# The eight products of a context group tied together, in a masked attention kernel

## The chip, the cores and the metric

The kernel runs on one core of one Trainium2 chip. The time is the device time of an execution in microseconds (us); the number given is the median of several runs. Besides, one execution was profiled.

## The reference

There are 16 batches of 512 features by 1024 tokens. Queries, keys and values are one and the same projection; a token mask removes keys from the softmax, and a masked query attends evenly to everything.

```python
xt = jnp.transpose(x, (0, 2, 1))                       # x: (16, 512, 1024)
q = xt @ Wq.T
qh = q.reshape(B, T, NH, dk).transpose(0, 2, 1, 3)     # NH = 8, dk = 64
scores = scale * jnp.einsum('bhqd,bhkd->bhqk', qh, qh)
logits = (scores * cmask + (1.0 - cmask) * NEG) * rmask
attn = jax.nn.softmax(logits, axis=-1)
ctx = jnp.einsum('bhqk,bhkd->bhqd', attn, qh)
ctx = ctx.transpose(0, 2, 1, 3).reshape(B, T, D)
return x + jnp.transpose(ctx @ Wo.T, (0, 2, 1))
```

## The kernel before

**Compaction.** About half of the tokens of a batch are unmasked. The kernel sorts token numbers into slots, unmasked first, and computes the attention for 544 slots alone: four blocks of 128 and a tail of 32. A masked token's output is the projected mean, which is added to its row elsewhere. Rows come and go by indirect DMAs on POOL's queue (`rows` L335, `scatter_now` L796).

**A batch on TensorE.** Rows are transposed (`xt`, L420) into `pm` tiles; ScalarE (ACT) rounds them to f16 (L380) and VectorE (DVE) takes the remainder (L381). The query projection (`query`, L443) is 12 f16 products for each of 8 tiles; its result is moved out by ACT (L446) and split into f16 halves. `value` (L489) transposes it to values. `scores` (L611) makes for one head and one block of keys a tile `pss` of 128 x 544 in four f16 products, and ACT turns it into the exponentials `p` with their sums (L615). The scores of the 32 tail slots are made for four heads at once (L586): 16 products whose weights are 32 columns wide, each head in a strip of its own of the array, followed by one exponential (L590), a split on DVE and transfers into `pt`. `attend` (L629) multiplies the exponentials with the values in f32: for a pair of heads and a block of keys four products, each 64 columns wide, the two heads in the two halves of the array. The tail's part of the context (L632) is four products at full width, after which ACT copies `pav` out (L636). `recip_rows` (L665) transposes the reciprocal sums into a `pm` tile, from which they go through DRAM to the rows of `rb`; `norm` scales with them, and `project` (L712, L717) makes the output rows.

**PSUM.** There are two buffers for score tiles (`ps_s`), two of the small ones (`ps_m`, whose tiles are `pm`) and one for the context (`ps_av`).

**The order of the work.** `run` writes the work out by hand. The loop runs over the 16 batches; in each there are 18 steps (`S`): 16 pairs (p, i) of a pair of heads p and a block i, and two for the tail. A step issues the scores of two heads, and between them `fill` puts in pieces of a list `m` of other work (transposes, queries and values of the next batch, output projection of the one before), by shares of a planned cost. Context work comes later: after i = 1 and i = 3 the `attend` calls of two earlier steps are made one after the other, the younger first. These are the eight products of a group:

```python
elif i in (1, 3):
    for f in ready[1::-1] + ready[2:]:
        f()
    ready = []
```

This is the order in which instructions are given to a scheduler, which chooses the order on each engine by priorities and by when it holds operands to be ready. The first call of a group begins with `i` odd and with the head k = 1. `behind(ins)` tells the scheduler to issue what is in its scope after `ins`; `high_priority(offset=HPO)`, with HPO = 300, ranks what is in its scope above other work. [...]

Of the kernel before, what the change touches and what calls it, by code (L numbers as in the profile page):

```python
# [23 lines left out]
DK = 64  # L24
# [8 lines left out]
CH = C // 2  # L33
# [13 lines left out]
HPO = 300  # L47


class Fast:  # L50
# [12 lines left out]
    def __init__(self, ctx, tc, x, x_nat, mask_t, wq_t, wo_t, out):  # L63
        self.tc, self.nc = tc, tc.nc
        self.x, self.x_nat, self.out = x, x_nat, out
        self.B = x.shape[0] // T
        pool = lambda name, bufs, **k: ctx.enter_context(tc.tile_pool(name=name, bufs=bufs, **k))
        self.const = pool("const", 1)
        self.one = pool("one", 1)
        self.dram = pool("dram", 8, space=bass.MemoryType.DRAM)  # L70
        self.ps_s = pool("ps_s", 2, space=PS)
        self.ps_av = pool("ps_av", 1, space=PS)
        self.ps_m = pool("ps_m", 2, space=PS)
        self.st = {}
        self.scatters = []
        self.exp, self.pool = [], []

        self.paced, self.beat = False, None
        self.urgent, self.spare = [], []

        self.soon = []
        self.w, self.raw = {}, {}
        self.src = {"q": wq_t, "o": wo_t}
        self.setup(mask_t)
# [535 lines left out]
    def attend(self, b, p, i, ps):  # L620
        nc, s = self.nc, self.st[b]

        if i == 1:
            s["pav"] = self.ps_av.tile([P, 2, 512], F32, tag="av", name="pav")
        for g in range(2):
            for k in (1, 0) if i < 4 else range(2):
                cols = slice(g * CH, (g + 1) * CH)
                if i < 4:
                    nc.tensor.matmul(s["pav"][k * DK:(k + 1) * DK, g, :CH], lhsT=s["v"][p][:, i, k * DK:(k + 1) * DK],  # L629
                                     rhs=ps[k][:, cols], start=(i == 1), stop=False)  # L630
                else:
                    nc.tensor.matmul(s["pav"][:, g, :CH], lhsT=s["vt"][p // 2][:, k, p % 2 * 2:p % 2 * 2 + 2, :],  # L632
                                     rhs=s["pt"][:, p % 2, cols], start=False, stop=(k == 1))
        if i == 4:
            c = self.sb([P, C], F32, "c", 4)
            nc.scalar.copy(c.rearrange("p (g c) -> p g c", g=2), s["pav"][:, :, :CH])  # L636
            s["c"].append(c)
# [192 lines left out]
    def run(self, flag):  # L830
# [7 lines left out]
        def xt(n):  # L838
            return [(0.45, L(self.xt, n, c)) for c in range(4)] + [(0.25, L(self.xt, n, 4))]

        def query(n, e, g):
            u = [(1.37, L(self.query, n, e, g))]
            return u + [(0, L(self.qsplit, n, e))] if g else u

        def value(n, e):
            return [(0.45, L(self.value, n, e))]
# [8 lines left out]
        for i, e in enumerate(ends):  # L855
            g = list(range(ends[i - 1] + 1 if i else 0, e + 1))
# [73 lines left out]
        if True:  # L930
            for b in range(B + 1):
# [18 lines left out]
                if n < B:  # L950
                    q, x, v = (lambda e, g: query(n, e, g)), xt(n)[2 if b == 0 else 0:], (lambda e: value(n, e))
# [19 lines left out]
                    if b == 0:  # L971
                        k = next(k for k, (c, f) in enumerate(m) if f is index[0][1])
# [32 lines left out]
                def fill(part, end=False):  # L1005
                    nonlocal done, goal, pos
                    goal += part * unit
                    while pos < len(m) and (end or (part and done + m[pos][0] / 2 <= goal)):
                        m[pos][1]()
                        done += m[pos][0]  # L1010
                        pos += 1

                for st, (p, i) in enumerate(S):
                    soon, self.soon = self.soon, []
                    for f in soon + free.get(st, []):
                        f()
                    if i is None:
                        self.scores(b, p, None)
                    else:
                        ps = [self.scores(b, 2 * p, i)]  # L1020
                        if i == 2 and whole:
                            whole.pop()()
                    fill(share[st][0], st == N - 1)
                    if i is not None:
                        ps.append(self.scores(b, 2 * p + 1, i))

                    for _ in range(1 if b < B - 2 else -(-len(self.urgent + self.spare) // (N - st))):
                        self.issue()

                    if i in (0, 2):  # L1030
                        ready, todo = todo, []
                    elif i in (1, 3):
                        for f in ready[1::-1] + ready[2:]:
                            f()
                        ready = []
                    fill(share[st][1])
                    if i is not None:
                        todo.append(L(self.attend, b, p, i, ps))
                    if i == 3:
                        (whole if p < 3 else todo).append(L(self.attend, b, p, 4, None))  # L1040
                        if p < 3:
                            free.setdefault(st + 2, []).append(L(self.recip_sums, b, p))
                            free.setdefault(st + 3, []).append(L(self.recip_rows, b, p))
                            if p < 2 or b == B - 1:
                                free.setdefault(min(st + 7, N - 1), []).append(L(self.norm, b, p))
# [148 lines left out]
```

## Time and profile before

| | |
|---|---|
| median of three runs | 1074.26 us (1073.34 to 1080.06) |
| profiled execution | 1082.2 us |
| its span, first to last instruction | 1080.5 us |
| TensorE (PE) busy | 1053.5 us, 98% |
| VectorE (DVE) busy | 739.3 us, 68% |
| ScalarE (ACT) busy | 679.0 us, 63% |
| GpSimd (POOL) busy | 317.5 us, 29% |
| granted TensorE clock, mean | 0.993 |

The profile names a group by source line, engine, operation and tiles (out<-in), with partitions x elements and type; x is the number of records. A record of a f32 context product is half of a product, so the 1024 products of L629 are 2048 records. A length in the timeline is that of a pipelined product from its issue to its end; what a product takes of TensorE is seen from start to next start. Idle time stands with the one who ended it.

### The profile page before, as it was taken

How to read it: one execution, taken by the hardware profiler on the slowest of the kernel's cores; microseconds unless marked ns; L12 is line 12 of the kernel's file. 1: busy time of each engine (PE TensorE's matmuls, PEld its weight loads, DVE VectorE, ACT ScalarE, POOL GpSimd, SP SyncE). 2: the span in 40 equal slices, each digit the busy share in tenths (PEclk: the TensorE clock that was granted, in tenths of full speed). 3: DMA queues.
4: the chain of work that ended last, by engine and by line, in shares of the span. 5: the costliest groups of instructions: out<-in, count | busy, mean ns of one | idle time of the engine just before them, and what ended most of it. 6: DMA issues, size and time to landing. Idle time of an engine off the chain costs nothing.

```text
span 1080.5 us, 23254 instructions
## 1 busy us (share of the span) xinstructions
PE 1053.5 (98%) x8386; PEld 698.3 (65%) x8386; DVE 739.3 (68%) x2375; ACT 679.0 (63%) x1722; POOL 317.5 (29%) x303
## 2 busy tenths in 40 slices
PE   7899999999999999999999999999999999999996
PEld 6566666666666666666666666666666676666553
DVE  5698668676765767767685676958577676757553
ACT  4786667566666756657666666766667565655550
POOL 2101022232401222332322323223232322234643
PEclk8999999999999999999999999999999999999999
DMA  5756565546655654666556566554765555466652
GB/s 186 218 152 167 138 175 157 170 139 191 173 141 156 170 168 145 189 192 172 175 143 194 168 182 188 154 172 134 211 190 171 179 149 154 134 179 195 193 165 85
DMA packets 78122, 181.35 MB, mean 168 GB/s; under 512 B 15008, under 2 KB 16800, under 8 KB 78000
## 3 DMA queue, kind: packets, MB, share of 16 engines
q1 hardware_dynamic: 56816, 111.62, 37.1%
q0 software_dynamic: 21184, 68.18, 19.8%
q8 instruction: 68, 1.11, 0.4%
q14 instruction: 54, 0.44, 0.1%
HBM read 92.34 MB, written 33.91 MB: 117 GB/s over the span
## 4 chain that ended last, share of the span: by engine, by line
PE 88%; DVE 5%; ACT 3%; issue 2%; DMA 1%; POOL 0%; another core or an unknown queue 0%; POOLq 0%; SPq 0%; ACTq 0%; DVEq 0%
PE pav L629 23%; PE pss L611 21%; PE pm L443 15%; PE pm L712 14%; PE pm L420 3%; PE pav L632 3%; PE pm L489 2%; PE pss L586 2%; PE pm L665 1%; ACT p L615 1%; PE pm L511 1%; ACT xm L365 1%; PE warm L303 1%; ACT p L590 1%; DVE p L596 1%
## 5 line engine op out<-in xcount | busy, mean ns | idle before, releaser
L615 ACT ACTIVATE p<-pss,nm 128x544 f32<-128x544 f32 x512 | 365.9, 717 | 231.8 <-PE pss L611 221.8
L611 PE MATMUL pss<-xx 128*128 128x272 f16 x2048 | 314.1, 280 | 3.2 <-ACT p L615 2.3
L629 PE MATMUL pav<-p,v 128*64 128x272 f32 x2048 | 273.5, 401 | 0.0
L611 PEld LDWEIGHTS <-xx 128*128 128x128 f16 x2048 | 193.1, 100 | 77.8 <-issue 31.3
L629 PEld LDWEIGHTS pav<-p,v 128*64 128x64 f32 x2048 | 131.9, 136 | 94.4 <-issue 34.0
L796 POOL DMA_INDIRECT y_out<-xa,idx x68 | 68.7, 1011 | 283.2 <-PE pss L611 83.9
L443 PE MATMUL pm<-xh,wqh 128*128 128x274 f16 (+1 forms) x512 | 143.7, 281 | 3.1 <-DVE xa L717 2.2
L443 PE MATMUL pm<-xh,wql 128*128 128x274 f16 (+1 forms) x512 | 143.2, 280 | 0.0
L443 PE MATMUL pm<-xl,wqh 128*128 128x274 f16 (+1 forms) x512 | 143.1, 280 | 0.0
L335 POOL DMA_INDIRECT xa<-x_in,idx x68 | 76.4, 1124 | 174.6 <-PE pss L611 64.4
L443 PEld LDWEIGHTS <-wqh 128*128 128x128 f16 x1024 | 99.1, 99 | 26.0 <-issue 7.1
L796 POOL DMA_INDIRECT y_out<-xi,idx x60 | 76.8, 1280 | 121.9 <-PE pss L611 43.3
L615 ACT ACTIVATION_READ_ACCUMULATOR p<-pss,nm 128x1 f32 x512 | 103.5, 202 | 0.0
L717 DVE SCALAR_TENSOR_TENSOR xa<-pm,xa 128x512 f32<-128x512 f32 x60 | 41.4, 690 | 87.7 <-PE pm L712 83.6
L335 POOL DMA_INDIRECT xi<-x_in,idx x60 | 62.1, 1036 | 109.8 <-PE pss L611 39.0
L712 PE MATMUL pm<-woh,ch 128*128 128x512 f16 x240 | 91.1, 379 | 0.0
L712 PE MATMUL pm<-woh,cl 128*128 128x512 f16 x240 | 91.0, 379 | 0.0
L712 PE MATMUL pm<-wol,ch 128*128 128x512 f16 x240 | 91.0, 379 | 0.0
L446 ACT ACTIVATE q<-pm 128x272 f32<-128x272 f32 (+1 forms) x128 | 50.6, 395 | 60.0 <-PE pm L443 52.5
L712 PEld LDWEIGHTS <-ch 128*128 128x128 f16 x480 | 46.4, 98 | 45.7 <-issue 1.3
L365 ACT ACTIVATE xm<-xm 128x1024 f32<-128x1024 f32 (+1 forms) x62 | 62.5, 1009 | 1.9 <-DMA xm<-x_nat_in 1.9
L783 DVE TENSOR_TENSOR xi<-xi,ub 128x512 f32<-128x512 f32 (+1 forms) x60 | 41.3, 691 | 30.5 <-PE pss L611 28.5
(191 smaller groups left out, 1562.5 us busy)
## 6 DMA issues: line engine op xcount, KB each, us to landing
xx<-hl SPq DMA_DIRECT2D x256, 136.0 KB
xm<-x_nat_in SPq DMA_DIRECT2D x56, 512.0 KB
rb<-rd SPq DMA_DIRECT2D x128, 136.0 KB
pt<-c SPq DMA_DIRECT2D x64, 136.0 KB
pt<-p SPq DMA_DIRECT2D x64, 136.0 KB
ub<-ud SPq DMA_DIRECT2D x16, 256.0 KB
xi<-x_nat_in SPq DMA_DIRECT2D x8, 256.0 KB
xa<-x_in,idx POOLq DMA_INDIRECT x68
```

The source lines that it names most:

```text
L335: dma = self.nc.gpsimd.indirect_dma_start(out=tile[:n], out_offset=None, in_=self.x, in_offset=bass.IndirectOffsetOnAxis(ap=idx, axis=0))
L365: self.nc.scalar.activation(s["xm"][k], s["xm"][k], AF.Copy, accum_out=s["ms2"][:, k:k + 1])
L420: self.pe = nc.tensor.transpose(pt[:, c, :], x[:n, c * P:(c + 1) * P], self.ident[:n, :n]).ins
L443: self.beat = nc.tensor.matmul(pq, lhsT=w[:, c, e * P:(e + 1) * P], rhs=xx[:, c, cols], start=(k == 0), stop=(k == 3 * DC - 1)).ins
L446: nc.scalar.activation(s["q"][:, e, cols], pq, AF.Copy, scale=1.0 / (SX * SW))
L611: self.beat = nc.tensor.matmul(pt[:, g, :CH], lhsT=xx[:, 2 * k, i * P:(i + 1) * P], rhs=xx[:, 2 * k + a, g * CH:(g + 1) * CH], start=(a == ...
L615: self.exp = [nc.scalar.activation(t.rearrange("p (g c) -> p g c", g=2), pt[:, :, :CH], AF.Exp, bias=s["nm"][p // HG][:, p % HG:p % HG + 1 ...
L629: nc.tensor.matmul(s["pav"][k * DK:(k + 1) * DK, g, :CH], lhsT=s["v"][p][:, i, k * DK:(k + 1) * DK], rhs=ps[k][:, cols], start=(i == 1), s ...
L712: nc.tensor.matmul(po[:cols.stop - cols.start], lhsT=a[:, e, cols], rhs=w[:, e, :], start=(e == 0 and k == 0), stop=(e == DC - 1 and k == 2))
L717: self.nc.vector.scalar_tensor_tensor(x, po, 1.0 / (SX * SW), x, ALU.mult, ALU.add)
L783: self.once(self.nc.vector.tensor_tensor(x[:n], x[:n], s["ub"][:n], ALU.add), self.beat)
L796: dma = self.nc.gpsimd.indirect_dma_start(out=self.out, out_offset=bass.IndirectOffsetOnAxis(ap=idx, axis=0), in_=x, in_offset=None)
```

## The change

The first product of a group is remembered in `group_first`. The seven others are issued behind it and at high priority. It is forgotten at the start of the next group, so the `attend` calls after the last group of the kernel still refer to that one.

```diff
         self.st = {}
+        self.group_first = None
         self.scatters = []
...
                 if i < 4:
-                    nc.tensor.matmul(s["pav"][k * DK:(k + 1) * DK, g, :CH], lhsT=s["v"][p][:, i, k * DK:(k + 1) * DK],
-                                     rhs=ps[k][:, cols], start=(i == 1), stop=False)
+                    with ExitStack() as st:
+                        if self.group_first:
+
+                            st.enter_context(self.behind(self.group_first))
+                            st.enter_context(self.tc.high_priority(offset=HPO))
+                        mm = nc.tensor.matmul(s["pav"][k * DK:(k + 1) * DK, g, :CH], lhsT=s["v"][p][:, i, k * DK:(k + 1) * DK],
+                                              rhs=ps[k][:, cols], start=(i == 1), stop=False)
+                    self.group_first = self.group_first or mm.ins
...
                     elif i in (1, 3):
+                        self.group_first = None
                         for f in ready[1::-1] + ready[2:]:
                             f()
```

## The prediction

> **What bounds the kernel.** I read the page's busy table and its chain of waits first, then the groups of TensorE, then a stretch of PE's timeline from the middle of the run. All sums are against the profiled execution: 1082.2 us, of which 1080.5 are span.
>
> ```profile
> PE 1053.5 (98%) x8386; PEld 698.3 (65%) x8386; DVE 739.3 (68%) x2375; ACT 679.0 (63%) x1722; POOL 317.5 (29%) x303
> ...
> PE 88%; DVE 5%; ACT 3%; issue 2%; DMA 1%; POOL 0%; another core or an unknown queue 0%; POOLq 0%; SPq 0%; ACTq 0%; DVEq 0%
> ...
> L611 PE MATMUL pss<-xx 128*128 128x272 f16 x2048 | 314.1, 280 | 3.2 <-ACT p L615 2.3
> L629 PE MATMUL pav<-p,v 128*64 128x272 f32 x2048 | 273.5, 401 | 0.0
> ```
>
> TensorE is busy 98% of the span, is 88% of the chain, and L629 waits 0.0 us for data. So the time is PE's own sequence, and two things count: what a change of the order costs inside that sequence, and whether the new order makes PE wait. The change alters neither the number nor the shape of any instruction.
>
> The timeline (start in us, length, engine, line, names, x records) shows what order is worth. A context product is two records, so x16 is a whole group of eight products, x8 four, x4 two.
>
> ```profile
> 488.02 1.09 PE L420 MATMUL pm<-ident,xa 128*128 128x128 f32 x8
> 488.95 0.63 PE L611 MATMUL pss<-xx 128*128 128x272 f16 x4
> 489.51 1.14 PE L629 MATMUL pav<-p,v 128*64 128x272 f32 x8
> 490.57 0.33 PE L665 MATMUL pm<-ident,rcol 128*128 128x128 f32 x1
> 490.83 0.68 PE L629 MATMUL pav<-p,v 128*64 128x272 f32 x4
> 491.44 0.43 PE L420 MATMUL pm<-ident,xt 32*128 32x32 f32 x4
> ...
> 493.80 0.65 PE L586 MATMUL pss<-xx 128*32 128x272 f16 x16
> 494.38 0.33 PE L540 MATMUL pm<-ident,smcol 128*128 128x128 f32 x1
> ...
> 495.95 0.63 PE L611 MATMUL pss<-xx 128*128 128x272 f16 x4
> 496.41 0.28 PE L549 MATMUL pm<-ident,m 128*128 128x4 f32 x2
> ...
> 499.31 0.63 PE L611 MATMUL pss<-xx 128*128 128x272 f16 x4
> 499.86 2.06 PE L629 MATMUL pav<-p,v 128*64 128x272 f32 x16
> 501.85 0.64 PE L611 MATMUL pss<-xx 128*128 128x272 f16 x4
> ```
>
> From start to next start, two products take 491.44 - 490.83 = 0.61 us, four 490.57 - 489.51 = 1.06, eight 501.85 - 499.86 = 1.99. That is 0.23 per product and 0.15 for each run. Entering costs too: four scores take 0.46 (495.95 to 496.41) ahead of a full-width product, but 0.56 (488.95 to 489.51) ahead of a context run. So **each separate run of these 64-column products costs 0.15 + 0.095 = 0.245 us** beyond its products.
>
> The same holds for the 32-column scores of the tail slots, L586. Sixteen take 494.38 - 493.80 = 0.58; they run four at a time, four slots of 0.116 as for other scores (0.46), so a run costs 0.12 and, entering alike, 0.21 in all.
>
> **The change, part by part.** I compared the orders in which the two built programs' instructions stand.
>
> *Groups made whole.* Before, 100 of the 128 groups stand whole and the L629 products form 174 runs; after, 127 stand whole and there are 128 runs. 46 runs fewer at 0.245: **-11.3 us**. Of these, 26 lie in the middle batches: 13 times the pattern above (two products; eight transposes and four scores; four; one L665; two) becomes one run. The other 20 lie in the first and last batches and in a few groups between.
>
> *What is pushed into other places.* In 12 of those 13 batches the order after the whole group is now: eight transposes, four scores, the four L632, L665, then L586 cut as **10, 3 and 3**, with four transposes and then twelve L443 in the cuts. Before, 16 stood together. Ten need three slots, the threes one each: five slots and three runs, 5 x 0.116 + 3 x 0.21 = 1.21, against 0.58 + 0.09 = 0.67. That is 0.54 a batch, 6.5 for twelve. One more batch is cut 9 and 7 around an L665 (five slots, two runs: 0.33). Together **+6.8 us**. The trace has no such cut in steady work; its bounds are 0 (a broken slot and its seams vanish beside the neighbour) and 8, and I take 6.8, because it is built from two neighbouring rows.
>
> *A wait for L665.* Its output needs one of the two pm buffers, and the one due to come free is held until DVE has split the first four transposes (L381). The weight load of L665 waited for that already:
>
> ```profile
> 488.75 1.11 ACT L380 ACTIVATE xh<-pm 128x512 f16<-128x512 f32 x2
> 489.41 1.29 DVE L381 SCALAR_TENSOR_TENSOR xl<-pm,xh 128x512 f16<-128x512 f32 x2
> 490.57 0.14 PEld L665 LDWEIGHTS pm<-ident,rcol 128*128 128x128 f32 x1 [0.41 <-DVE xl L381]
> ```
>
> The first of the two L381 (0.69 each) ends at 490.10, 2.08 after the transposes began at 488.02; L665 came at 2.55, hidden by four context products. In the new order only transposes (0.93), scores (0.46) and four L632 (some 0.50, from the L632 stretch that begins at 493.12) stand between: PE arrives at 1.89 and stands 0.2 us. Thirteen times: **+2.6 us**; bounds 0 (ACT begins its L380 earlier) and 6.5.
>
> *Start and end.* In the last batch nothing of a next one fills PE: between 1010 and 1030 us PE is busy 17.4 of 20, with waits of 1.69 and 0.87 us for exponentials. There the divided groups are filler between scores. After the change five score tiles follow one another once; an exponential takes 0.71 + 0.19 = 0.90 against 0.46 for its scores, with two buffers, so three of the five wait 0.44 each, 1.3. The first batches lose filler likewise; I estimate another 1.7 from the same price. **+3 us**, bounds 0 and 5.
>
> *The tie itself.* It is in the scheduler's order and not a semaphore. The group begins with the younger pair of p tiles and the later head, so its first product waits for the newest data and the seven behind it for nothing newer. What ranks below them is held at most 2 us: exponentials in the middle, covered while ACT is idle 37% of the span. DVE and ACT swap a few neighbours in order; POOL's order is unchanged and SP's moves in a dozen places, all off PE's path.
>
> Sum: -11.3 + 6.8 + 2.6 + 3 = **+1.1 us**: 1083.3 for the profiled execution's 1082.2, and 1075.4 from the median of 1074.26.
>
> [...] Counting every change between full, 64- and 32-column products gives 399 before and 363 after. [...] The rows say 0.245 us per context run and show that a broken slot costs again: -4.5 for both terms. I go by the rows.
>
> **Rivals.**
> *Only the seams count.* The cut L586 and L665 cost nothing, since the pieces stand among products that keep the array fed; the edges cost 3. Then -11.3 + 3 = -8.3, 1066 us; with free edges too, 1063. For it: all 46 runs surely go. Against it: the L586 row shows a run's price plainly, and L665's slack was under half a microsecond.
> *Slower: late tail scores.* The last L586 comes after twelve L443 and four transposes more: 1.4 + 0.44 + 0.54 of cuts, some 2.3 us. Its exponential (L590) stands in ACT's queue ahead of the next L446 eviction and scores' exponentials, and holds one of the two score buffers meanwhile; it decides once the delay passes the work that PE has without them. That work is L540, three scores and then twelve L443 (1.4 us), so I expect it hidden. If half of 1.9 us comes through in 12 batches, +11 makes 1087. The tail's own consumer is safe: L590 at 494.50, its last transfer issued by 497.99, the next L632 at 511.04.
> *The order is not what was meant.* Excluded for the groups: 127 of 128 are whole.
>
> **How the numbers follow.** Near nothing 0.74, seams only 0.14, late tail scores 0.12. About 1% (10.7 us) is what a measurement of this kernel can tell from no change; the three runs before lie 6.7 apart. Seams only is mostly within 1%, a third of it beyond: 0.06 for faster. Late tail scores are nearly all slower: 0.12. With each unknown term at its end the sum runs from -8.3 (seams only, edges at 3) to +8.2 (-11.3 + 8 + 6.5 + 5), which from the median is 1066 to 1082.5 us: the range. It leaves out the late tail scores and the far end of seams only.
>
> **What would show it.** The changed profile should have L629 in x16 rows nearly everywhere, with two products still 0.23 apart; L586 rows of x10, x3, x3; L665 straight after L632, with a short PE wait for DVE's L381. L586's busy time should rise and that of PE in all stay within some 5 us. PE waits for L590 or L615 in the middle batches would make the slower rival right; L586 pieces that add nothing to the start-to-start times would make the faster one right.

## The result, and the profile after

The changed kernel took 1082.72 us in the median of nine runs (1079.08 to 1085.71), the kernel before 1078.21 us in nine (1073.34 to 1080.06). The ratio is **1.0051, 95% interval 1.0034 to 1.0067**: slower by 5.5 us (3.7 to 7.2), where the forecast was +1.1 us. In another session the same changed kernel gave 1.0058. Ratios below are each against runs of the kernel before on the same chip; a thousandth is 1.08 us. The first four experiments ran on one chip, the next four on a second and the last four on a third. One run of the kernel before, of 2672.38 us, is left out of the ratios of the first four.

The profiled execution of the changed kernel took 1080.61 us, of which 1078.9 are span, and so happens to be shorter than that of before (1082.2). A part of this is at the start: the granted clock of before's execution was half (0.50) from 14.9 to 21.7 us and from 42.2 to 45.6 us, and in the changed one it was full (1.00) in both stretches. The ratio decides what the change is worth; the traces are read for where, stretch by stretch. The page, lines as shown of before:

```profile
PE 1049.4 (97%) x8386; PEld 702.5 (65%) x8386; DVE 737.0 (68%) x2375; ACT 674.8 (63%) x1722; POOL 318.6 (30%) x303
...
PE 84%; DVE 6%; ACT 4%; DMA 3%; issue 2%; POOL 0%; POOLq 0%; SPq 0%; DVEq 0%; ACTq 0%
...
L612 PE MATMUL pss<-xx 128*128 128x272 f16 x2048 | 314.9, 280 | 2.3 <-ACT p L616 2.2
L635 PE MATMUL pav<-p,v 128*64 128x272 f32 x2048 | 262.9, 399 | 0.0
```

The context products (L635, L629 of before) are 10.6 us less busy, 262.9 for 273.5, as runs of them went from 174 to 128. But PE's share of the chain fell from 88% to 84%, and that of DMA rose from 1% to 3%: in some place the path has left TensorE. (Lines of the changed kernel stand 1 to 7 higher: L665 is L672, L586 is L587, L632 is L639, L696 is L703, L659 is L666, L381 is L382.)

**The middle of the run** looks as foreseen. PE's timeline, from a whole context group to the end of the tail's scores:

```profile
482.04 2.05 PE L635 MATMUL pav<-p,v 128*64 128x272 f32 x16
484.02 1.09 PE L421 MATMUL pm<-ident,xa 128*128 128x128 f32 x8
484.95 0.63 PE L612 MATMUL pss<-xx 128*128 128x272 f16 x4
485.33 0.75 PE L639 MATMUL pav<-pt,vt 128*128 128x272 f32 x4
486.09 0.33 PE L672 MATMUL pm<-ident,rcol 128*128 128x128 f32 x1
486.35 0.53 PE L587 MATMUL pss<-xx 128*32 128x272 f16 x10
486.81 0.43 PE L421 MATMUL pm<-ident,xt 32*128 32x32 f32 x4
487.17 0.30 PE L587 MATMUL pss<-xx 128*32 128x272 f16 x3
...
488.89 0.29 PE L587 MATMUL pss<-xx 128*32 128x272 f16 x3
489.12 0.33 PE L541 MATMUL pm<-ident,smcol 128*128 128x128 f32 x1
```

The group is one row of x16, L672 follows L639, and the tail's scores are cut 10, 3 and 3. From the group's first product to L541 there are 489.12 - 482.04 = 7.08 us. Before, the same work began with two products of the divided group,

```profile
487.41 0.68 PE L629 MATMUL pav<-p,v 128*64 128x272 f32 x4
```

and took 6.97 us, to the L540 at 494.38 that the prediction shows. So a middle batch lost 0.1 us, where the prediction's terms made +0.25 (two runs fewer, -0.49; the cuts, +0.54; the wait, +0.2).

**The last batch** does not look as foreseen. PE's waits from 985 us on:

```profile
PE pm L672 <- DVE rcol L666: 4.8, 1, 4.8
PE pss L612 <- ACT p L616: 0.5, 2, 0.3
```

Each row gives the total, the number of waits and the longest. Once, and for 4.8 us, PE stands at L672, the transpose of the reciprocal sums, for DVE. There is no such row among the waits of before:

```profile
PE pss L611 <- ACT p L615: 1.7, 1, 1.7
PE pm L443 <- DVE xa L717: 1.1, 1, 1.1
PE pss L611 <- ACT c L636: 0.9, 1, 0.9
```

The timeline around it, first of before (L673 issues the transfer of `rb`, L659 is the last operation on the reciprocals, L696 multiplies `c` with `rb`):

```profile
1016.14 1.10 SPq L673 DMA_DIRECT2D rb<-rd  x2
1018.41 0.17 DVE L659 TENSOR_TENSOR rcol<-rcol,hit 128x10 f32<-128x10 f32 x1
1021.25 0.33 PE L665 MATMUL pm<-ident,rcol 128*128 128x128 f32 x1
1022.41 0.73 DVE L696 TENSOR_TENSOR c<-c,rb 128x544 f32<-128x544 f32 x1 [2.60 <-issue]
```

and then of the changed kernel:

```profile
1009.71 1.10 SPq L680 DMA_DIRECT2D rb<-rd  x2
...
1010.73 0.16 DVE L658 TENSOR_TENSOR rcol<-z,corr 128x8 f32<-128x8 f32 x1
...
1016.16 0.72 DVE L703 TENSOR_TENSOR c<-c,rb 128x544 f32<-128x544 f32 x1 [4.67 <-DMA rb<-rd]
...
1017.70 0.16 DVE L664 TENSOR_SCALAR rcol<-rcol 128x10 f32<-128x10 f32 x1
...
1018.24 0.21 DVE L665 RECIPROCAL rcol<-rcol 128x10 f32<-128x10 f32 x1
...
1019.06 0.16 DVE L666 TENSOR_TENSOR rcol<-rcol,hit 128x10 f32<-128x10 f32 x1
...
1019.28 0.33 PE L672 MATMUL pm<-ident,rcol 128*128 128x128 f32 x1 [4.76 <-DVE rcol L666]
```

Before, DVE finished the reciprocals of this batch (L659) and then came to L696, which belongs to the batch before. After, L703 stands **between** two operations on the reciprocals, L658 and L664. It waits 4.67 us for `rb`. L664, whose input L658 had left at 1010.89, begins at 1017.70, 6.81 us later and behind L703, and L665 and L666 follow it (1018.24 and 1019.06): here DVE kept the order of the program. The chain of work shows the same from its start, each piece with its start and length:

```profile
1004.86 4.79 DMA rd<-rr
...
1010.23 5.84 DMA rb<-rd
...
1016.16 0.72 DVE c L703
...
1019.14 0.09 DVE rcol L666
...
1019.28 0.33 PE pm L672
```

Two transfers of 4.79 and 5.84 us, through DRAM and back, are on the path that sets the end. Behind the stand the clock is lower. These are the busy times of the engines in one stretch, the clock (PEclk) third from the end, of the changed kernel and then of before:

```profile
1019.00:1023.00 4.00, 3.72 (x13) 1.86 (x14) 0.50 (x3) 1.61 (x4) 2.80 (x3) 0.58 0.41 115
```

```profile
1019.00:1023.00 4.00, 4.00 (x31) 2.51 (x31) 1.40 (x3) 1.61 (x4) 3.09 (x4) 1.00 0.96 306
```

At 0.58 for 4.00 us, 1.7 us of TensorE's work is lost besides. Stand and clock, 4.76 + 1.7, less the 1.7 and 0.9 us that PE stood before in this part of the batch, are 3.9 us: most of the loss, if the reading is right. That was tried.

### The profile page after: what moved, and what is told of

Same layout as the page of the kernel before. It is cut to its first block, busy times and chain, and to the rows that moved or that the text cites. A ratio compares the mean times of both kernels' runs of the same rounds, so it can differ in the third digit from the quotient of the medians.

```text
span 1078.9 us, 23256 instructions
## 1 busy us (share of the span) xinstructions
PE 1049.4 (97%) x8386; PEld 702.5 (65%) x8386; DVE 737.0 (68%) x2375; ACT 674.8 (63%) x1722; POOL 318.6 (30%) x303
## 4 chain that ended last, share of the span: by engine, by line
PE 84%; DVE 6%; ACT 4%; DMA 3%; issue 2%; POOL 0%; POOLq 0%; SPq 0%; DVEq 0%; ACTq 0%
PE pav L635 22%; PE pss L612 20%; PE pm L719 15%; PE pm L444 15%; PE pm L421 3%; PE pav L639 3%; PE pm L490 2%; PE pss L587 2%; PE pm L672 2%; ACT p L616 1%; ACT xm L366 1%; DMA rb<-rd 1%; PE pm L512 1%; DMA rd<-rr 1%; DMA xx<-hl 1%
## 5 line engine op out<-in xcount | busy, mean ns | idle before, releaser
L616 ACT ACTIVATE p<-pss,nm 128x544 f32<-128x544 f32 x512 | 365.7, 717 | 235.3 <-PE pss L612 229.0
L635 PE MATMUL pav<-p,v 128*64 128x272 f32 x2048 | 262.9, 399 | 0.0
L635 PEld LDWEIGHTS pav<-p,v 128*64 128x64 f32 x2048 | 135.7, 136 | 94.2 <-issue 27.2
L616 ACT ACTIVATION_READ_ACCUMULATOR p<-pss,nm 128x1 f32 x512 | 103.6, 202 | 0.0
L719 PE MATMUL pm<-woh,ch 128*128 128x512 f16 x240 | 91.5, 381 | 0.0
L719 PE MATMUL pm<-wol,ch 128*128 128x512 f16 x240 | 91.5, 381 | 0.0
L719 PE MATMUL pm<-woh,cl 128*128 128x512 f16 x240 | 91.4, 381 | 0.0
L719 PEld LDWEIGHTS <-ch 128*128 128x128 f16 x480 | 46.8, 98 | 46.4 <-issue 2.4
L382 DVE SCALAR_TENSOR_TENSOR xl<-pm,xh 128x512 f16<-128x512 f32 (+1 forms) x75 | 43.1, 607 | 26.7 <-ACT xh L381 26.7
```

Source lines behind the costliest of these rows:

```text
L382: self.xs = nc.vector.scalar_tensor_tensor(self.xl[dst], src, SX, self.xh[dst], ALU.mult, ALU.subtract).ins
L616: self.exp = [nc.scalar.activation(t.rearrange("p (g c) -> p g c", g=2), pt[:, :, :CH], AF.Exp, bias=s["nm"][p // HG][:, p % HG:p % HG + 1 ...
L635: mm = nc.tensor.matmul(s["pav"][k * DK:(k + 1) * DK, g, :CH], lhsT=s["v"][p][:, i, k * DK:(k + 1) * DK], rhs=ps[k][:, cols], start=(i == ...
L719: nc.tensor.matmul(po[:cols.stop - cols.start], lhsT=a[:, e, cols], rhs=w[:, e, :], start=(e == 0 and k == 0), stop=(e == DC - 1 and k == 2))
```

## The experiments

### Where the loss sits: without the last batch, and the last batch alone

Theory A: the last batch makes the loss, by L703 ahead of the reciprocals. Rival: it is spread over the batches, in cuts and waits.

```diff
-                        if self.group_first:
+                        if self.group_first and b < self.B - 1:       # not_last
+                        if self.group_first and b == self.B - 1:      # only_last
```

> The change in every batch but the last: 134 context runs instead of 128, the cut tail scores stay. Theory A (the loss sits in the last batch, where VectorE's new order puts the multiplication by rb ahead of the reciprocals that L672 needs, so TensorE stands 4.8 us and then gets half its clock for 3.4 us): ratio to before 0.998 to 1.000, since start (-1.7 us) and middle (+0.8 us) together are about -1. Theory B (the loss is the cut tail scores and the short L672 waits of the middle batches, 12 to 13 times 0.4 us): 1.004 to 1.005, as the whole change.

> The change in the last batch alone: 168 context runs, all tail scores whole. Theory A: slower by 4 to 6.5 us, ratio 1.004 to 1.006, with a wait of about 5 us for L672 in the last batch. Theory B: within 1 us of before, ratio 0.999 to 1.001.

Measured: not_last **1.0015** (1.0007 to 1.0024), only_last **1.0043** (1.0030 to 1.0057). Fifteen batches lose 1.6 us between them, where theory A had a gain or nothing; one batch loses 4.6. The wait of 5 us at L672 that was expected of only_last is not in its profile as such:

```profile
PE pss L612 <- ACT p L616: 3.7, 3, 3.2
...
PE pm L672 <- DVE rcol L666: 1.1, 1, 1.1
```

L666 was late there too (1025.87), but PE had just stood 3.2 us at scores, for an exponential, so that only 1.1 us was left to wait.

### The reciprocals ahead again, and the tail's scores whole

In sums_ahead the sums of head pair 0 of the last batch are given out one step earlier and L703 of the batch before is issued behind the last operation on them. In tail_tied the 16 scores of the tail are tied as the context products are, in all batches but the first.

```diff
-        nc.vector.tensor_tensor(m, m, self.hit[:, b, :].unsqueeze(1).broadcast_to([P, 2, 5]), ALU.mult)
+        self.sums = b, nc.vector.tensor_tensor(m, m, self.hit[:, b, :].unsqueeze(1).broadcast_to([P, 2, 5]), ALU.mult).ins
...
-        self.once(nc.vector.tensor_tensor(c, c, s["rb"][p], ALU.mult), self.beat if p < 3 else None)
+        with self.behind(*(self.sums[1:] if b == self.B - 2 and p == 3 and self.sums[0] == b + 1 else ())):
+            self.once(nc.vector.tensor_tensor(c, c, s["rb"][p], ALU.mult), self.beat if p < 3 else None)
...
-                            free.setdefault(st + 2, []).append(L(self.recip_sums, b, p))
+                            free.setdefault(st + (2 if b < B - 1 or p else 1), []).append(L(self.recip_sums, b, p))
```

```diff
+            first = None
...
+                        with ExitStack() as st:
+                            if first and b:
+                                st.enter_context(self.behind(first))
+                                st.enter_context(self.tc.high_priority(offset=HPO))
+                            self.beat = nc.tensor.matmul(pt[r * CT:(r + 1) * CT, g, :CH], lhsT=xx[:, 2 * k, 512:C],
+                                                         rhs=xx[:, 2 * k + a, g * CH:(g + 1) * CH],
+                                                         start=(a == 0), stop=(a == 1)).ins
+                        first = first or self.beat
```

> The changed kernel, with the reciprocals of the first pair of heads of the last batch given out one step earlier and the multiplication by rb of the batch before issued behind them. TensorE's order is that of the changed kernel but for L672, which stands 3 places earlier. Theory A: the wait of 4.8 us is gone and no half clock follows, so 5 to 6 us faster than the change, ratio to before 0.998 to 1.001. Theory B: 1.004 to 1.005. If the multiplication was only where the wait showed and the next one takes its place: in between, 1.002 to 1.004.

> The changed kernel with the 16 tail scores tied in the same manner: 128 context runs and 34 runs of tail scores, as many of the latter as before the change. The wait in the last batch stays. By the prediction's price of a cut (0.54 us a batch, 0.33 once) it is 6 to 7 us faster than the change, ratio to before 0.998 to 0.999. If the cuts cost nothing, 1.005 as the change; if tying moves the wait for the first transposes into the gap, 1.000 to 1.003.

Measured: sums_ahead **1.0025** (1.0016 to 1.0035), tail_tied **1.0024** (1.0013 to 1.0034). Each takes back about half. For sums_ahead that was less than I expected of theory A, and its profile had a stand of 3.5 us for an exponential (L616) at the scores that follow, and they ran slower: four took 1.06 us, against 0.62 us for four at 1015.71. So the question was open whether the wait had only moved on: perhaps the context products that used to stand between scores are what is missing there. tail_tied is far from the 0.998 to 0.999 that the prediction's price of a cut made. Its stretch of PE's timeline that is shown above for the changed kernel (L635 is L641 here, and L587 is L592) was:

```profile
487.57 2.06 PE L641 MATMUL pav<-p,v 128*64 128x272 f32 x16
...
491.89 0.65 PE L592 MATMUL pss<-xx 128*32 128x272 f16 x16
492.47 0.43 PE L421 MATMUL pm<-ident,xt 32*128 32x32 f32 x4
...
494.30 0.33 PE L541 MATMUL pm<-ident,smcol 128*128 128x128 f32 x1
```

494.30 - 487.57 = 6.73 us for 7.08: in this stretch the cuts cost 0.35 us a batch, not 0.54. Over the whole of this batch, from one L541 to the next but one, the two kernels are nearer: 63.15 us in tail_tied, 63.36 in the changed kernel, 63.25 before. Tying the tail's scores costs something in the other half of the batch.

### Two groups of the last batch

PE's order in the last batch differs from before above all in the two groups of head pair 0, so the tie was put there alone, and everywhere else; the latter also with tail_tied's edit, and the whole change with both edits.

```diff
-                        if self.group_first:
+                        if self.group_first and (b, p) == (self.B - 1, 0):    # two_groups
+                        if self.group_first and (b, p) != (self.B - 1, 0):    # all_but_two, tails_but_two
```

> The change for two groups alone, those of the first pair of heads in the last batch: 170 context runs against 174, tail scores whole. If the loss of the last batch sits there (these two lose the scores that stood between their products, and VectorE's order is the bad one), as much as the change in the whole last batch cost: ratio to before 1.003 to 1.005. If it is spread over that batch's groups: 1.001 to 1.002.

> The change for every group but those two: 132 context runs, VectorE's order in the last batch as before the change. If the two groups hold the loss: 1.000 to 1.002, what the change without the last batch gave (1.0015) or a microsecond better, for four more runs saved. If the loss is spread: 1.003 to 1.004.

> As the run before, and the 16 tail scores tied as well: 132 context runs, 34 runs of tail scores. The traces of the middle batches show 4.75 us instead of 5.10 from the eight transposes to the L540 product when the tail scores are whole, so 0.35 a batch: ratio 0.997 to 0.999, the first version faster than before. If gains don't add: 1.000 to 1.002.

> The changed kernel with the tail scores tied and the reciprocals of the last batch ahead of the multiplication by rb. Each alone took about half of the loss away (1.0024 and 1.0025 against 1.0051). If they add: 0.999 to 1.001. If the reciprocals' place only moves the wait to the scores that follow: 1.001 to 1.002.

Measured: two_groups **1.0031** (1.0018 to 1.0043), all_but_two **1.0009** (1.0001 to 1.0018), tails_but_two **0.9994** (0.9981 to 1.0006), both **1.0018** (1.0009 to 1.0027). Two of 128 groups make most of the loss. In the profile of two_groups PE does not wait at L672 at all. L666 came at 1023.92, but PE stood at scores until 1024.23:

```profile
PE pss L612 <- ACT p L616: 3.8, 2, 3.5
```

The other 126 groups make +1.0 us. With the tail's scores whole as well, the kernel can't be told from the one before; no version was measurably faster than it. The run both came out where it was expected if the wait only moves, between 1.001 and 1.002: its profile again has PE standing at scores, for 1.9 us and 1.2 us more.

### DVE's order or the missing filler

These two groups change two things at once: scores follow one another without context products between them, and L703 is ahead of the reciprocals. The orders of the built kernels part them. The tie on the first group alone brings the bad order on DVE with the second group still divided; on the second group alone it leaves DVE's order as before; and sums_two is two_groups with the edit of sums_ahead: both groups whole, reciprocals ahead.

```diff
-                        if self.group_first:
+                        if self.group_first and (b, p) == (self.B - 1, 0) and i < 2:     # first_group
+                        if self.group_first and (b, p) == (self.B - 1, 0) and i >= 2:    # second_group
+                        if self.group_first and (b, p) == (self.B - 1, 0):    # sums_two, with sums_ahead's edit
```

> The tie applies to one group of the whole kernel alone: i < 2 of head pair 0 in the last batch. PE's order there is AV8 S8 m S12 AV2 S8 AV6 S4 AT2 L672 AT2 S4, so the second group stays partly divided, while DVE's order is the one of the changed kernel: the product of c and rb (L703) stands ahead of the reciprocals (L665). Theory A, that DVE's order makes the loss: 1.002 to 1.004 of the kernel before. Rival, that the lost filler between scores makes it: about half of two_groups' loss, 1.001 to 1.002.

> The tie applies to the other of those two groups alone: i >= 2 of head pair 0 in the last batch. PE's order is AV2 S8 m AV2 S4 AV4 S8 AV8 S8 L672 AT3 S4 AT1 S4, and DVE's order is as in the kernel before, with the reciprocals ahead of L703. Theory A, DVE's order: 0.999 to 1.001. Rival, lost filler: 1.001 to 1.002.

> two_groups, with the reciprocals of head pair 0 of the last batch given out a step earlier and L703 of the batch before issued behind them, as in sums_ahead: both groups whole, DVE's order as in the kernel before. Theory A, DVE's order: 0.999 to 1.001. Rival, lost filler: 1.002 to 1.003, with the stand of PE at the scores (L612, for exponentials) and not at L672.

> The changed kernel again, to have its ratio on the same chip as these three: 1.004 to 1.006 by what was measured of it; the profile should again have PE standing at L672 for DVE's L666 by 4 to 5 us, with half the clock behind it.

Measured: first_group **1.0048** (1.0029 to 1.0067), second_group **1.0003** (0.9988 to 1.0017), sums_two **1.0007** (0.9995 to 1.0019), after_again **1.0058** (1.0041 to 1.0076). The tie on one group of 128 costs all that the whole change costs, within the intervals, and somewhat more than theory A had (1.002 to 1.004). The waits of PE from 985 us on, of first_group:

```profile
PE pm L672 <- DVE rcol L666: 4.6, 1, 4.6
```

and of sums_two (its lines stand one higher from L703 on), where L672 is not among them:

```profile
PE pss L612 <- ACT p L616: 0.5, 2, 0.3
PE pm L720 <- DVE ch L707: 0.5, 1, 0.5
PE pm L720 <- DVE cl L708: 0.3, 1, 0.3
```

In second_group the transfer of `rb` was as late as ever:

```profile
1014.68 0.17 DVE L666 TENSOR_TENSOR rcol<-rcol,hit 128x10 f32<-128x10 f32 x1
...
1017.60 0.27 PE L672 MATMUL pm<-ident,rcol 128*128 128x128 f32 x1
1020.83 0.72 DVE L703 TENSOR_TENSOR c<-c,rb 128x544 f32<-128x544 f32 x1 [4.75 <-DMA rb<-rd]
```

L703 waits 4.75 us there too, but L666 is done 6 us before it, and L672 has its data when PE comes to it. The wait comes through only at L719, where PE stands 1.3 us for `ch`:

```profile
PE pm L719 <- DVE ch L706: 1.3, 1, 1.3
```

So it is not the late transfer that decides, and not the missing filler, but what stands behind L703 in DVE's queue. The missing filler is what sums_two keeps: 0.8 us (-0.5 to 2.0). Its edit also moves L672 three places ahead on PE, but there L672 would wait longer for DVE, not shorter. That the tie on the first group moves L703 and that on the second doesn't is read from the orders of the built programs; by what rule of the scheduler it does was not followed up.

One measure can be taken of every trace: from the first context product of head pair 0 in the last batch to that of head pair 1 stand the same 95 records of TensorE in all of these kernels.

| order on DVE | kernels | from start to start, us (one execution each) |
|---|---|---|
| reciprocals first, as before | before, second_group, all_but_two, tails_but_two, not_last | 16.6, 15.1, 17.4, 15.5, 17.3 |
| reciprocals first by sums_ahead's edit | sums_two, sums_ahead, both | 15.0, 18.7, 18.2 |
| L703 first | changed, after_again, first_group, two_groups, only_last, tail_tied | 20.4, 20.6, 20.9, 18.7, 20.7, 19.8 |

The means of the first and the last row are 16.4 and 20.2: 3.8 us. These rows mix chips. On the third chip alone it is 20.6 and 20.9 against 15.1 and 15.0; on the first, 20.7 and 19.8 against 17.3 and 18.7; on the second, 18.7 against 17.4, 15.5 and 18.2. In each of the eight profiles from the first two chips PE stands once for 1.7 to 3.5 us at scores; in the four from the third, no stand at scores is above 0.3 us. So the stand at L672 is seen plainly in the changed kernel, first_group and after_again alone (4.8, 4.6 and 4.3 us). In only_last, tail_tied and two_groups L666 was as late, but that other stand hid the wait in part or whole, and their profiles can't say how much of the loss is whose.

sums_ahead and both show that this stretch can be long with the reciprocals first, by a late exponential. In sums_two the order of TensorE in it is the same as in sums_ahead, and it took 15.0; so the order alone does not bring that stand. It ran on another chip, though. The ratio of sums_ahead, 1.0025, is about that of sums_two and not_last together (0.7 + 1.5 thousandths); a moved wait is not needed for it, and not excluded either. For both, sums_two and tails_but_two together make 1.0001; that it measured 1.0018 stays open.

## Why the prediction was wrong

Of the 7.3 us between the forecast 1075.4 and the measured 1082.72, 4.0 are the kernel before itself: 1074.26 was the median of the first three of its runs, 1078.21 that of all nine. The rest is the change. Its 5.5 us lie within the ends that the prediction gave, -8.3 and +8.2, but by luck: those were the ends of other terms. And nine runs could tell 0.5%, where the prediction had held that less than 1% can't be told.

**The tie itself: wrong, and this is the step that failed.** "DVE and ACT swap a few neighbours in order; POOL's order is unchanged and SP's moves in a dozen places, all off PE's path." The first half was right, the last words weren't looked into. One of these few swaps put an operation that waits for a transfer ahead of three short ones that TensorE needs next. Cost taken: 0. Shown: 5.2 us by first_group (3.1 to 7.2), while second_group, without that swap, is at 0.3 (-1.3 to 1.8), and sums_two, with both groups tied and the reciprocals ahead again, at 0.8. The trace of before held all that was needed: `rb` was issued at 1016.14 and L696 began at 1022.41, 6.27 us later, with the reciprocals (L657 to L659, 0.63 us on the timeline, 1017.95 to 1018.58) ahead of it. Operations put behind L696 would have been that late.

**Groups made whole, -11.3: right in the number of runs, not shown in size.** 128 runs are left, and their busy time is 10.6 us less; but busy time is not elapsed time. In the middle stretch of tail_tied, with two runs fewer and no cut, 0.24 us is gained, where the prediction's prices make 0.29. Over the kernel the gain does not come through: tails_but_two has 42 runs fewer and no new cut, which with the waits for L672 and the first batches' filler makes -10.3 + 2.6 + 1.7 = -6.0, and it measured -0.6 us (-2.1 to 0.6). Part of the gap is what tying the tails costs in the other half of a batch; the rest stays open.

**Cut tail scores, +6.8: too high.** By the stretches shown a cut batch costs 0.35 us and not 0.54, so twelve cost 4.2. From start to next start the pieces of ten and three take 0.46, 0.23 and 0.23 us, 0.92 in all against the 0.58 of the whole sixteen: the slots and the price of a run were right. The entry price of 0.09, added for each of the two extra pieces, does not show. Busy time of these scores rose by 6.2 us (L587 27.7, from 21.5) and overstates the cost. In the runs, tails_but_two against all_but_two gives back 1.6 us, with the two intervals together anything from 0 to 3.2.

**The wait for L672, +2.6: right in kind, its size not shown.** In the stretch above L672 begins 2.07 us after the transposes (484.02 to 486.09), as 1.89 and a stand of 0.2 make, and its weight load was held by DVE's L382 for 0.23 us:

```profile
486.09 0.14 PEld L672 LDWEIGHTS pm<-ident,rcol 128*128 128x128 f32 x1 [0.23 <-DVE xl L382]
```

But the row of all 64 L672 has little of it as idle time of PE, 5.1 us of which 4.8 are the one stand in the last batch:

```profile
L672 PE MATMUL pm<-ident,rcol 128*128 128x128 f32 x64 | 20.7, 324 | 5.1 <-DVE rcol L666 4.8
```

**Start and end, +3: right in kind.** For the last batch 1.3 was taken and sums_two shows 0.8 with its interval reaching from -0.5 to 2.0. Of the two waits of before that the prediction put down to exponentials, only that of 1.69 us was one; the other stands in the row of waits as 0.9 us for L636, the copy of `pav`. The first batches were not tried by themselves.

The four terms without the tie summed to +1.1 us, and all_but_two, the change without the two groups, measured +1.0 (0.1 to 1.9); for the two groups the sum had next to nothing (four runs fewer, -1.0, and the filler, +1.3). That agreement is in part luck: the cuts were taken 2.6 us too dear, and the gain from whole groups came short as well. The term put at nothing was worth more than four times the sum of the rest.

**The rivals.** Neither came about. "Only the seams" fails by the cuts, which cost 0.35 each in their stretch, and by the measured time. "Late tail scores" fails by the waits: no L590 or L615 exponential is among PE's waits in the middle batches (of the changed kernel, from 125 to 940 us), and fifteen batches lose 1.6 us, where that rival added 11. The slower rival had the right sign, but the delay was looked for on ACT; it was on DVE, where the prediction had itself named the swap.

**The price of a run** came by the rows to -4.5 us for groups and cuts together. In the middle stretch two context runs fewer are -0.5 by it; tail_tied gained 0.24 with the wait for L672 in it. Over the kernel the gain fell short of the rows' price, as said above. Whether a part of the price goes with a change between full, 64- and 32-column products, of which the prediction counts 36 fewer, no run shows.

## What to carry to other kernels

When an order is changed by a scheduler's hint, list every swap on every engine, above all at the ends of the run, and ask of each instruction that moved forward what it waits for, and of those now behind it who waits for them. A wait can cost little in one place of a queue and its whole length in the next, though no instruction was added or lengthened: L703 waited 4.75 us in second_group, and PE stood 1.3 us for `ch`; it waited 4.67 us in the changed kernel, and PE stood 4.76 us at L672. Terms for the steady part may be nearly right and still be less than one such place: a tie limited to where its order is harmless (all_but_two) keeps them apart. Here that alone did not make the kernel faster than before.

## What was not expected of the hardware

**Small transfers took long.** `rd` (10 rows) took 4.79 us and `rb` 5.84 us in the chain of the changed kernel, 4.06 and 6.54 us in that of first_group. Together it is 10 us and more from the reciprocals to their rows.

**The clock after a stand.** In the changed kernel half the clock (0.50) was granted for 3.41 us behind the stand of 4.76 us, from 1019.68 us on. In first_group the mean clock was 0.72 from 1014 to 1019 us and 0.50 from 1019 to 1023, which makes an estimated 6.8 us of half clock, and this began while PE still stood (at some 1016.2, where PE went on at 1018.48). In after_again too L672, the first product behind the stand, was already slow: 0.47 us, against 0.33 us at 1009.38. The listed waits alone do not settle when this comes. not_last had a mean clock of 0.57 from 1021 to 1025 us, an estimated 3.4 us at half, with no PE wait above 1.9 us; in all_but_two the four scores behind a wait of 1.7 us took 0.62 us, as four did at full clock in the changed kernel (at 1010.05). Whether PE really worked between the listed waits can't be told, as the next point shows.

**Late completions.** In before's trace, four products of L611 are listed from 1013.30 to 1013.94; ACT and DVE, which waited for scores, both went on at 1016.41, 2.5 us after that end, and POOL at 1016.65. sums_ahead and two_groups have the like, with 3.10 and 3.15 us: in two_groups eight products are listed to end at 1020.22, and the exponential that waited for them began at 1023.37. This is what the late exponentials of these three traces go back to. No run was made for its cause, and it stays open.
